# Two graph layers on one core: transfers of the reciprocals split by rows, divisions two steps later, values in pieces

## The chip, the cores and the metric

The kernel runs on one core of a Trainium2 chip. The metric is the device time of one launch in microseconds. The core has five engines with one instruction stream each: TensorE (PE in the profile; PEld is its weight load), VectorE (DVE), ScalarE (ACT), GpSimd (POOL, hardly used here) and SyncE (SP), which here only issues DMA transfers. All transfers run on the core's 16 DMA engines. [...]

## The reference, cut to what matters

Two graph layers run in sequence on `x` of shape (8, 2048, 256), with one adjacency matrix of 2048 x 2048. Each layer is followed by a residual sum and a layer norm.

```
# layer 0, 8 heads of 32 columns, per batch entry
x_proj = x @ W[h];  e = leaky_relu(e_src[i] + e_dst[j], 0.2) + beta * log(adj + 1e-6)
attn   = softmax(where(adj > 0, e, -inf))           # over j
x      = layernorm(x + concat_h(attn @ x_proj) @ W_out.T)
# layer 1, one head of 256 columns
e      = leaky_relu((x W1) (x W2)^T, 0.2);  attn = softmax(where(adj > 0, e, -1e12))
x      = layernorm(x + relu(attn @ (x W3)))
```

What the change touches is the softmax of layer 0. The kernel sums unnormalised products and denominators and divides at the end, by multiplying with the reciprocal of the denominator.

## The kernel before, in words

A batch entry of layer 0 is an object of class `Gat`. It goes through its work in 64 **steps**: four head pairs (`hp`) times 16 column tiles (`jt`) of 128. A step (`Gat.step`) takes a tile `mt` of the transposed edge weights (128 x 2048, 1 MB, loaded from DRAM by `load_mt`), makes one score tile `s` per head on VectorE (L373), and lets TensorE multiply: `val` with the projected values `v`, `den` with the column factors `re` (both L408, in `products`). In some steps the denominator part is added on VectorE instead (L384). There are four buffers for `s`, so VectorE can be two steps ahead of TensorE.

After a head pair's last step, `Gat.finish` takes over. It is a generator: each `yield` ends what is done in one step, and `step` takes the next part of each generator in the list `later` at its start. The parts are: copy the sums out of PSUM (L421, L424); after two steps bring the denominators into a compact shape (`rc`, L428) and take reciprocals (L429); a step later store them to DRAM (`rec_d`, L432). Every second head pair (`lo` is not 0) then has reciprocals of four heads complete, and a step later it brings them back, each row of 1024 broadcast over the 32 partitions of its head, as `rb` (L440, one transfer of 128 x 1024 for each half of the rows), and multiplies the 128 x 1024 halves of `ht` with it (L443). In entry 0 nothing is put off: all parts are run through at once.

There are thus 16 places (8 entries, second and fourth head pair) with two `rb` transfers and two divisions each.

Layer 1 of an entry is an object of class `Dot`, with 16 steps of 128 rows: scores `e` (L530), mask and row maximum on VectorE (L535), exponential on ScalarE (L538), turned blocks (L553, L555), product with `h3` (L569), relu, residual sum and norm (L574, L575, `layer_norm`).

The main loop at the bottom runs layer 1 of one entry together with the steps of the next entry's layer 0. `dot.step(fill)` calls `fill` at three places, and there `layer_0(n)` does n steps. At an entry's end the loop runs the last two dot steps of the entry before, then `output` (product with `W_out`, residual sum, norm; L469 to L482) and `turn` (transposes and `h3`) of the new one, with two steps in each gap. Entry 0 runs beside `others`, a generator that projects the `x` of all other entries (`row`, L270), in the order 2, 3, 4, 5, 1, 6, 7, and stores the values of entries 2 to 7 in DRAM (`v_d`). They are fetched back by `load` (L310) when the entry begins. `others` has two buffers for the values it makes, `v` and `h3`; entries 6 and 7 both use `h3`.

What sets the order: TensorE follows the program's order from the start, and SyncE from line 650 on (all but entry 0), so a SyncE transfer that waits for a buffer holds up the ones after it. The order of VectorE and ScalarE is laid out ahead of time by a planner that works with its own estimates of durations and keeps to it, whatever really comes first.

Buffers with a common tag share slots. The tag `ht` of pool `chunk` has three, for `dn`, `rb`, layer 1's `h1`, the `x` groups of `output` and, in layer 1 of entry 0, the adjacency rows (L212). The tag `d` of pool `wide` has two of 128 x 2048: odd `mt` tiles in entry 0 and in entry 1's first head pair, and later the sums of L384.

Of the kernel before, what the change touches and what calls it, by code (L numbers as in the profile page):

```python
# [9 lines left out]
F32 = mybir.dt.float32  # L10
# [8 lines left out]
P = 128  # L19
# [8 lines left out]
def kernel(  # L28
# [26 lines left out]
    nc = tc.nc  # L55
    B, N, D = x.shape
    H, _, DH = w_proj.shape
    NT = N // P
    KC = D // P
    BK = 512  # L60
    NB = N // BK
    HALF = N // 2
    HP = 2
    NP = H // HP
    IG = BK // P
# [9 lines left out]
    chunk = ctx.enter_context(tc.tile_pool(name="chunk", bufs=2))  # L75
# [4 lines left out]
    def mm_tile(name):  # L80
        return ps.tile([P, BK], F32, tag="mm", name=name)

    def wide_tile(name, tag, bufs, dtype=F32):
        return wide.tile([P, N], dtype, tag=tag, name=name, bufs=bufs)
# [75 lines left out]
    v_d = dram.tile([B, P, NT, D], F32, name="v_d")  # L160
    re_d = dram.tile([B, P, 2, NT, H], F32, name="re_d")
    rec_d = dram.tile([B, NP // 2, 2, 2, 2, HALF], F32, name="rec_d")
    x1_d = dram.tile([B, N, D], F32, name="x1_d")

    def load_x(b, g):

        xg = wide.tile([P, IG, D], F32, tag="pen", name="xg", bufs=1)
        nc.sync.dma_start(xg, x[b].rearrange("(t p) d -> p t d", p=P)[:, ts(g, IG), :])
        return xg
# [64 lines left out]
    class Gat:  # L234
# [72 lines left out]

        def load(self):
            self.v = whole.tile([P, NT, D], F32, name="v")
            nc.sync.dma_start(self.v, v_d[self.b])  # L310

        def load_factors(self):
            self.re = small.tile([P, 2, NT, H], F32, name="re", bufs=3)
# [98 lines left out]
        def finish(self, hp):  # L412

            b, lo = self.b, hp % 2 * HP * DH
            if hp == 0:
                self.ht = whole.tile([P, NT, KC, P], F32, tag="heads", name="ht")
            ht = self.ht[:, :, hp // 2, :]
            for s in range(2):  # L420
                nc.scalar.copy(ht[lo:lo + HP * DH, ts(s, NT // 2), :],  # L421
                               self.val[ts(s, HP * DH), :].rearrange("p (t i) -> p t i", i=P))
            dn = chunk.tile([P, HALF], F32, tag="ht", name="dn", bufs=3)
            nc.scalar.copy(dn, self.den)  # L424
            yield
            yield
            rc = small.tile([P, HALF // DH], F32, name="rc", bufs=1)
            nc.sync.dma_start(rc, dn[::DH, :].rearrange("q (p c) -> q p c", c=HALF // DH))  # L428
            nc.vector.reciprocal(rc, rc)  # L429
            yield  # L430
            for s in range(2):
                nc.sync.dma_start(rec_d[b, hp // 2, s, hp % 2].rearrange("a (p c) -> (a p) c", c=HALF // DH),  # L432
                                  rc[ts(s, HP * DH), :])
            if lo == 0:
                return
            yield
            for s in range(2):
                rb = chunk.tile([P, HALF], F32, tag="ht", name="rb", bufs=3)
                src = rec_d[b, hp // 2, s]
                nc.sync.dma_start(rb, bass.AP(tensor=src.tensor, offset=src.offset,  # L440
                                              ap=[[HALF, 2 * HP], [0, DH], [1, HALF]]))
                half = ht[:, ts(s, NT // 2), :]
                nc.vector.tensor_mul(half, half, rb.rearrange("p (t i) -> p t i", i=P))  # L443

        def output(self):


            b = self.b
            xb = x[b].rearrange("(t p) d -> p t d", p=P)
            xs = []  # L450

            def load(g):
                xs.append(chunk.tile([P, IG, D], F32, tag="ht", name="xg", bufs=3))
                nc.sync.dma_start(xs[g], xb[:, ts(g, IG), :])

            for g in range(NB - 1):
                load(g)
            yield
            for g in range(NB):
                if g == 2:  # L460
                    load(NB - 1)
                st = small.tile([P, IG, nc.vector.BN_STATS_DIM], F32, name="st4", bufs=1)
                mv = small.tile([P, IG, nc.vector.BN_AGGR_DIM], F32, name="mv4", bufs=2)
                z = self.ht[:, ts(g, IG)].rearrange("p t k i -> p t (k i)")
                for k in range(0, IG, 2):
                    y = mm_tile("y").rearrange("p (t c) -> p t c", t=2)
                    for i in range(2):
                        for kc in range(KC):
                            nc.tensor.matmul(y[:, i, :], self.ht[:, g * IG + k + i, kc, :], wot[:, kc, :],  # L469
                                             start=(kc == 0), stop=(kc == KC - 1))  # L470
                    nc.vector.tensor_add(z[:, k:k + 2, :], y, xs[g][:, k:k + 2, :])
                    for i in range(k, k + 2):
                        nc.vector.bn_stats(st[:, i, :], z[:, i, :])
                        nc.vector.bn_aggr(mv[:, i, :], st[:, i, :])
                f = small.tile([P, 2, IG], F32, name="f4", bufs=2)
                nc.scalar.activation(f[:, 0, :], mv[:, :, 1], AF.Ln, bias=eps_ln)
                nc.scalar.activation(f[:, 0, :], f[:, 0, :], AF.Exp, scale=-0.5)
                nc.vector.scalar_tensor_tensor(f[:, 1, :], mv[:, :, 0], -1.0, f[:, 0, :], ALU.mult, ALU.mult)
                for k in range(IG):
                    nc.scalar.activation(z[:, k, :], z[:, k, :], AF.Identity, bias=f[:, 1, k:k + 1],  # L480
                                         scale=f[:, 0, k:k + 1])
                nc.scalar.dma_start(x1_d[b].rearrange("(t p) d -> p t d", p=P)[:, ts(g, IG), :], z)  # L482
                yield
# [115 lines left out]
    def others():  # L599


        order = gats[2:-2] + gats[1:2] + gats[-2:]
        groups = [(gat, g) for gat in order for g in range(NB)]
        xgs, xts = [], []

        def load(n):
            if n < len(groups):
                xgs.append(load_x(groups[n][0].b, groups[n][1]))

        def turn(n):  # L610
            if n < len(groups):
                xts.append(chunk.tile([P, KC, BK], F32, tag="ht", name="xt", bufs=3))
                transpose_x(xgs[n], xts[n])
                load(n + 1)

        load(0)
        turn(0)
        for n, (gat, g) in enumerate(groups):
            turn(n + 1)
            if g == 0:  # L620
                gat.begin("h3" if n // NB % 2 or gat is order[-1] else "v")
            for k in range(IG):
                gat.row(g * IG + k, xts[n])
                if g == NB - 1 and k == IG - 1:
                    gat.factors()
                    for i in range(NB):
                        gat.scale(i)
                    if gat.b > 1:
                        gat.store()
                if g == 0 and k == IG - 1 and n > 0:  # L630
                    groups[n - 1][0].queries()
                yield
        order[-1].queries()
        yield

    projections, weights = others(), later_weights()
    count = (B - 1) * NT
    for k in range(1, NP * NT + 1):
        g0.step()
        if k == NP * NT:  # L640
# [11 lines left out]
    for b in range(1, B + 1):  # L652
        gat, fresh = gats[b - 1], gats[b] if b < B else None

        def layer_0(count):
            if fresh:
                fresh.step(count)

        if b > 1 and fresh:
            fresh.load()  # L660
            fresh.follow(gat)
        rows, turns = gat.output(), gat.turn()
        if dot is None:
            layer_0(4)
            next(rows)
            next(projections)
            layer_0(2)
        else:

            dot.step(lambda k: layer_0((0, 2, 2)[k]))  # L670
            if not fresh:
                for work in gat.later:
                    for _ in work:
                        pass

            def fill(k):
                if k == 1:
                    layer_0(2)
                    next(rows)

            dot.step(fill)

        for g in range(NB + 2):
            if g < NB:
                next(rows)
            if g > 1:
                next(turns)
                next(turns)
            if g < NB + 1:
                layer_0(2)  # L690
        dot = Dot(gat)
        dot.step(lambda k: layer_0((2, 0, 2)[k]))
        count = NP * NT - 20
        for i in range(NT - 3):
            n = (i + 1) * count // (NT - 3) - i * count // (NT - 3)
            dot.step(lambda k: layer_0((0, n - 2, 2)[k]))
# [31 lines left out]
```

## Time and profile before

| | before |
|---|---|
| time, median of 3 runs | 4535.02 us (4534.83 to 4538.08) |
| span of the profiled run | 4539.9 us |
| TensorE busy | 4289.9 us (94%) |
| VectorE busy | 3602.1 us (79%) |
| ScalarE busy | 1660.3 us (37%) |
| granted TensorE clock, mean | 0.978 |
| `mt` loads | 496 of 1024 KB |
| `rb` loads | 32 of 512 KB |
| `v` loads | 6 of 2048 KB |

How to read the lines. A group's line gives line, engine, operation, the tile written and those read, shapes and count, then busy time and mean duration in ns, then the idle time of the engine just before these instructions and what ended it. A line of the timeline gives start and duration in us, and in brackets the idle time before with what ended it. In the table by stretch, each engine's busy time is followed by its instruction count in brackets, and the last three columns are the granted clock of TensorE, the busy share of the 16 DMA engines, and GB/s. A busy TensorE is not TensorE at its peak, for the end of a matmul is modelled, and at half clock the same work shows twice the busy time.

### The profile page before, as it was taken

What the parts mean: (1) busy time and instruction counts of PE and PEld (TensorE: products, weight loads), DVE (VectorE), ACT (ScalarE), POOL (GpSimd) and SP (SyncE); (2) the same over time, 40 slices, a digit from 0 to 9 for tenths busy, and PEclk for the clock granted to TensorE, in tenths of its full rate; (3) what the DMA queues carried; (4) which work ended last, traced back from release to release, by engine and by line L of the source; (5) the groups of instructions that cost most, each with busy time, mean ns of one, the idle gap of its engine ahead of it and who ended that gap; (6) DMA issues with size and microseconds to landing.
All of it is one profiled execution on the core that took longest, in us unless ns stands there. A gap on an engine that the chain in (4) does not pass through costs nothing.

```text
span 4539.9 us, 59623 instructions
## 1 busy us (share of the span) xinstructions
PE 4289.9 (94%) x25072; PEld 2221.2 (49%) x25072; DVE 3602.1 (79%) x2606; ACT 1660.3 (37%) x3019; POOL 9.5 (0%) x14
## 2 busy tenths in 40 slices
PE   7989899998999989998999989999999989999899
PEld 4444354444544445454454444454454544544666
DVE  6878877897789879898789977898798987899222
ACT  6522133332333323333343323333333323333454
POOL 0000000000000000000000000000000000000000
PEclk9999899999999999999999999999999999999999
DMA  8877656555455554555545454455544455453211
GB/s 253 295 245 265 244 191 204 216 201 203 167 183 187 200 201 151 180 187 201 187 176 187 167 202 174 178 188 197 198 170 165 178 206 182 177 182 141 74 49 40
DMA packets 248652, 839.07 MB, mean 185 GB/s; under 512 B 30016, under 2 KB 148544, under 8 KB 173120
## 3 DMA queue, kind: packets, MB, share of 16 engines
q1 hardware_dynamic: 213056, 801.71, 49.9%
q10 hardware_dynamic: 35328, 33.56, 2.2%
q8 instruction: 196, 3.21, 0.3%
q14 instruction: 72, 0.59, 0.0%
HBM read 761.53 MB, written 73.14 MB: 184 GB/s over the span
## 4 chain that ended last, share of the span: by engine, by line
PE 47%; DVE 20%; DMA 10%; issue 8%; ACT 3%; SPq 0%; DVEq 0%; ACTq 0%
DVE s L373 13%; PE e L530 12%; PE acc L569 12%; PE val L408 9%; PE den L408 6%; DMA rb<-rec_d 5%; DMA mt<-mt_d 4%; DVE d L384 3%; PE pt L553 3%; PE h1p L520 2%; PE h3p L500 2%; DVE p L535 1%; PE y L469 1%; ACT d L390 1%; ACT p L538 1%
## 5 line engine op out<-in xcount | busy, mean ns | idle before, releaser
L373 DVE SCALAR_TENSOR_TENSOR s<-c,re,mt 128x2048 f32<-128x2048 f32 x1024 | 2354.6, 2342 | 205.7 <-PE den L408 147.1
L408 PE MATMUL val<-s,v 128*32 128x512 f32 x8192 | 1064.0, 613 | 136.6 <-DVE s L373 134.6
L569 PE MATMUL acc<-h,pts 128*128 128x256 f32 x4096 | 956.4, 381 | 26.8 <-ACT pts L555 26.8
L530 PE MATMUL e<-x1t,h 128*128 128x512 f32 x2048 | 909.4, 596 | 16.4 <-ACT pts L555 7.7
L569 PEld LDWEIGHTS acc<-h,pts 128*128 128x128 f32 x4096 | 748.2, 190 | 125.1 <-ACT pts L555 39.2
L408 PE MATMUL den<-s,re 128*32 128x512 f32 x5648 | 712.7, 598 | 0.0
L408 PEld LDWEIGHTS val<-s,v 128*32 128x32 f32 x8192 | 245.7, 111 | 788.0 <-issue 520.7
L384 DVE SCALAR_TENSOR_TENSOR d<-s,re,d 128x2048 f32<-128x2048 f32 x264 | 615.0, 2344 | 0.0
L530 PEld LDWEIGHTS e<-x1t,h 128*128 128x128 f32 x2048 | 380.3, 191 | 472.6 <-issue 414.8
L555 ACT COPY pts<-pt 128x512 f32<-128x512 f32 x512 | 296.1, 582 | 766.1 <-PE pt L553 758.7
L535 DVE CUSTOM_DVE_ANT_0 p<-p,pen 128x2048 f32<-128x2048 f32 x128 | 292.8, 2287 | 249.6 <-ACT p L532 237.8
L532 ACT ACTIVATE p<-e 128x512 f32<-128x512 f32 x512 | 302.9, 595 | 440.6 <-PE e L530 433.2
L408 PEld LDWEIGHTS den<-s,re 128*32 128x32 f32 x5648 | 194.0, 111 | 432.1 <-issue 427.4
L553 PEld LDWEIGHTS pt<-ident,p 128*128 128x128 f32 x2048 | 239.5, 141 | 229.0 <-issue 180.4
L538 ACT ACTIVATE p<-p,neg 128x2048 f32<-128x2048 f32 x128 | 256.7, 2005 | 234.6 <-DVE neg L535 234.6
L553 PE MATMUL pt<-ident,p 128*128 128x128 f32 x2048 | 320.6, 279 | 5.1 <-ACT p L538 5.1
L574 ACT ACTIVATE z<-acc,rec 128x256 f32<-128x256 f32 x128 | 60.6, 473 | 393.2 <-PE acc L569 274.3
L575 DVE TENSOR_TENSOR z<-z,x1r 128x256 f32<-128x256 f32 x128 | 54.0, 422 | 164.5 <-ACT z L574 164.3
L443 DVE TENSOR_TENSOR ht<-ht,rb 128x1024 f32<-128x1024 f32 x32 | 39.2, 1225 | 155.2 <-DMA rb<-rec_d 155.2
L270 PE MATMUL proj<-wp,xt 128*128 128x272 f32 (+1 forms) x512 | 135.8, 409 | 19.8 <-ACT both L274 10.1
L500 PE MATMUL h3p<-w3s,x1t 128*128 128x256 f32 x512 | 123.3, 384 | 14.2 <-ACT x1t L495 13.7
L224 ACT ACTIVATE f<-mv,eps_ln 128x1 f32<-128x1 f32 x128 | 37.8, 295 | 250.1 <-DVE mv L222 250.0
(89 smaller groups left out, 2016.3 us busy)
## 6 DMA issues: line engine op xcount, KB each, us to landing
mt<-mt_d SPq DMA_DIRECT2D x496, 1024.0 KB
c<-c_d SPq DMA_DIRECT2D x64, 1024.0 KB
pen<-pen_d SPq DMA_DIRECT2D x112, 512.0 KB
xg<-in_x_dram SPq DMA_DIRECT2D x60, 512.0 KB
adj_t<-in_adj_dram SPq DMA_DIRECT2D x16, 1024.0 KB
mt_d<-mt SPq DMA_DIRECT2D x16, 1024.0 KB
rb<-rec_d SPq DMA_DIRECT2D x32, 512.0 KB
x_d<-ht ACTq DMA_DIRECT2D x32, 512.0 KB
```

Source lines behind the costliest of these rows:

```text
L270: nc.tensor.matmul(t[:, 0:cols], xt[:, kc, ts(it % IG, P)], wp[:, kc, 0:cols], start=(kc == 0), stop=(kc == KC - 1))
L373: nc.vector.scalar_tensor_tensor(sa, self.cs[a], self.re[:, 0, jt, h:h + 1], mt, ALU.max, ALU.mult)
L384: nc.vector.scalar_tensor_tensor(d, sa, e[:, jt - 1, h:h + 1], d, ALU.mult, ALU.add)
L408: nc.tensor.matmul(dst[ts(q, DH), ts(c, BK)], weights[q % 2], s[q % 2][:, ds(q // 2 * HALF + c * BK, BK)], start=start, stop=stop)
L500: nc.tensor.matmul(t[:, ts(i, D)], x1t[:, kc, ts(2 * (j - 1) + i, P)], w3s[:, kc, :], start=(kc == 0), stop=(kc == KC - 1))
L530: nc.tensor.matmul(t, self.h1[:, kc, ts(it % IG, P)], self.x1t[:, kc, ts(c, BK)], start=(kc == 0), stop=(kc == KC - 1))
L532: nc.scalar.activation(p[:, ts(c, BK)], t, AF.Prelu, alpha=ALPHA)
L535: nc.vector.tensor_tensor_reduce(p, p, pen, -1.0, FMAX, ALU.add, ALU.min, neg)
L538: nc.scalar.activation(p, p, AF.Exp, bias=neg, scale=-1.0, accum_out=den)
L553: nc.tensor.transpose(t[:, ts(k, P)], p[:, ts(g * IG + k, P)], ident)
L555: nc.scalar.copy(pt, t)
L569: nc.tensor.matmul(acc, now[:, ts(k, P)], self.h3[:, j, :], start=(j == 0), stop=(j == NT - 1))
```

## The change

Five edits, all about when things are fetched and used:

1. **Reciprocals in four transfers a half.** Instead of one transfer of 128 x 1024 with a source of four rows, each repeated 32 times, there are four, each of one row to the 32 partitions of its head. In entry 0 the tile is taken from the tag `d` instead of `ht`.
2. **Divisions two steps behind.** The transfers of half 0 are issued in one step, those of half 1 in the next, then the divisions follow in one step each.
3. **Values in four pieces.** `load` becomes a generator; the first 512 KB are asked for at once, the others one a step.
4. **The x groups of `output`** are asked for one ahead instead of three at the start.
5. **Entry 0.** The first `x` group of `others` is asked for before the first step; the transposes of the next group come after the second row of the present one; ahead of entry 7 there are four turns with no row, so that entry 6's values can be stored first. The counts of steps are fitted to that.

```
         def load(self):
             self.v = whole.tile([P, NT, D], F32, name="v")
-            nc.sync.dma_start(self.v, v_d[self.b])
+            for g in range(NB):
+                nc.sync.dma_start(self.v[:, ts(g, IG), :], v_d[self.b, :, ts(g, IG), :])
+                yield
...
             yield
+            rbs = []
             for s in range(2):
-                rb = chunk.tile([P, HALF], F32, tag="ht", name="rb", bufs=3)
-                src = rec_d[b, hp // 2, s]
-                nc.sync.dma_start(rb, bass.AP(tensor=src.tensor, offset=src.offset,
-                                              ap=[[HALF, 2 * HP], [0, DH], [1, HALF]]))
+                if b == 0:
+                    rb = wide_tile("rb", "d", 2)[:, 0:HALF]
+                else:
+                    rb = chunk.tile([P, HALF], F32, tag="ht", name="rb", bufs=3)
+                for a in range(2 * HP):
+                    nc.sync.dma_start(rb[ts(a, DH), :],
+                                      rec_d[b, hp // 2, s, a // HP, a % HP:a % HP + 1, :].to_broadcast([DH, HALF]))
+                rbs.append(rb)
+                yield
+            for s, rb in enumerate(rbs):
                 half = ht[:, ts(s, NT // 2), :]
                 nc.vector.tensor_mul(half, half, rb.rearrange("p (t i) -> p t i", i=P))
+                yield
...
-            for g in range(NB - 1):
-                load(g)
+            load(0)
+            load(1)
             yield
             for g in range(NB):
-                if g == 2:
-                    load(NB - 1)
+                if 0 < g < NB - 1:
+                    load(g + 1)
...
         load(0)
+        yield
         turn(0)
         for n, (gat, g) in enumerate(groups):
-            turn(n + 1)
             if g == 0:
+                if gat is order[-1]:
+                    for _ in range(IG):
+                        yield
                 gat.begin("h3" if n // NB % 2 or gat is order[-1] else "v")
             for k in range(IG):
                 gat.row(g * IG + k, xts[n])
+                if k == 1:
+                    turn(n + 1)
...
-    count = (B - 1) * NT
+    next(projections)
+    count = (B - 1) * NT + IG
...
         if b > 1 and fresh:
-            fresh.load()
             fresh.follow(gat)
+            values = fresh.load()
+            next(values)
+            fresh.later.append(values)
...
             layer_0(4)
             next(rows)
             next(projections)
-            layer_0(2)
...
-        count = NP * NT - 20
+        count = NP * NT - (18 if b == 1 else 20)
```

## The prediction

> **What bounds the kernel now.** I read the page first, for the engines and the idle time:
>
> ```profile
> PE 4289.9 (94%) x25072; PEld 2221.2 (49%) x25072; DVE 3602.1 (79%) x2606; ACT 1660.3 (37%) x3019; POOL 9.5 (0%) x14
> ...
> PE 47%; DVE 20%; DMA 10%; issue 8%; ACT 3%; SPq 0%; DVEq 0%; ACTq 0%
> DVE s L373 13%; PE e L530 12%; PE acc L569 12%; PE val L408 9%; PE den L408 6%; DMA rb<-rec_d 5%; DMA mt<-mt_d 4%; DVE d L384 3%; PE pt L553 3%; PE h1p L520 2%; PE h3p L500 2%; DVE p L535 1%; PE y L469 1%; ACT d L390 1%; ACT p L538 1%
> ...
> L443 DVE TENSOR_TENSOR ht<-ht,rb 128x1024 f32<-128x1024 f32 x32 | 39.2, 1225 | 155.2 <-DMA rb<-rec_d 155.2
> ```
>
> TensorE (PE) is the bound: 4540 - 4290 = 250 us of its span are idle, so no change of waits alone can save much more than that. The chain spends 5% in the transfers of the reciprocals, `rb<-rec_d`. The last line says how: all 32 divisions (L443) found VectorE (DVE) idle in front of them, 155.2 us in sum, each time for that transfer. VectorE time is not TensorE time, so I went to the timeline of one such place, the end of entry 2's last head pair: VectorE, then TensorE, then the DMA share by stretch.
>
> ```profile
> 1580.24 0.15 DVE L572 RECIPROCAL rec<-den 128x1 f32<-128x1 f32 x1
> 1590.41 1.23 DVE L443 TENSOR_TENSOR ht<-ht,rb 128x1024 f32<-128x1024 f32 x1 [10.01 <-DMA rb<-rec_d]
> 1591.55 0.42 DVE L575 TENSOR_TENSOR z<-z,x1r 128x256 f32<-128x256 f32 x1
> 1591.89 2.35 DVE L373 SCALAR_TENSOR_TENSOR s<-c,re,mt 128x2048 f32<-128x2048 f32 x1
> 1595.48 1.23 DVE L443 TENSOR_TENSOR ht<-ht,rb 128x1024 f32<-128x1024 f32 x1 [1.24 <-DMA rb<-rec_d]
> ```
>
> ```profile
> 1594.29 1.91 PE L408 MATMUL val<-s,v 128*32 128x512 f32 x2 [6.33 <-DVE s L373]
> 1599.35 4.13 PE L408 MATMUL val<-s,v 128*32 128x512 f32 x16 [3.15 <-DVE s L373]
> ```
>
> ```profile
> 1576.25 1.23 SPq L440 DMA_DIRECT2D rb<-rec_d  x2
> ```
>
> ```profile
> 1588.00:1592.00 4.00, 0.00 (x0) 0.00 (x0) 1.59 (x3) 0.58 (x1) 0.00 (x0) 1.00 0.28 87
> 1592.00:1596.00 4.00, 1.71 (x2) 0.18 (x2) 2.76 (x2) 0.00 (x0) 0.00 (x0) 0.62 0.26 108
> ```
>
> The two transfers of 512 KB are issued at 1576.25 and only landed for the division at 1595.48, 19 us later. VectorE stands in program order in front of the divisions, the score tiles (L373) queue behind them, and TensorE waits 6.33 + 3.15 us for those. The last three columns are granted clock, DMA share and GB/s: while only `rb` is under way, the DMA share is 0.26 to 0.28, about 4 engines of 16, at 108 GB/s. The clock falls to 0.62: TensorE restarts at half clock after the gap. (On the page the clock is 0.978 on average; if the other state is 0.5, 0.022 / 0.5 x 4540 = 200 us run at half clock.)
>
> **What the Trainium skill says.** "DMA: Bandwidth & Descriptors", section "Why a DMA increments its semaphore by 16 and not by 1": a transfer uses the largest count of engines up to 16 that divides the slowest dimension of both sides. The old source leads with 4 rows, the destination with 128 partitions: 4 engines. The trace agrees (0.26 of 16). The new ones lead with 32 on both sides: 16 engines. The same page, "Rules for kernel authors", advises against cutting a transfer by partitions, because the parts share the same engines; that does not hold against a whole that is confined to four. "TensorE: Matmul & The Clock Gate", section "HAM oscillation — how this bites in real kernels", puts the price of a gap at half of the throttled time; the trace shows the halved clock at 1592 to 1600.
>
> **The change part by part.**
>
> *Reciprocals on 16 engines.* 1 MB in 2 transfers at 108 GB/s is 9.7 us alone, and 19 us as it shares its four engines with `mt`. On sixteen, at 4 x 108 = 432 GB/s, it is 1.2 us a half, plus a landing delay: the 8 KB `rec_d` stores issued to 1574.8 released the `rb` issue at 1576.25, so 1.5 us. SyncE (SP) issues 8 instead of 2 transfers; the price of one is between 0.32 us (`mt`) and 0.56 us (`rb`), so 2.6 to 4.5 us a pair. I take 0.5. The first half should land by about 1576.3 + 2 + 1.2 + 1.5 = 1581.
>
> *Divisions two steps behind.* The division of half 0 now comes after the score tiles of the next two steps. One step of L373 is 4.6 us, so it stands at about 1580.3 + 4.6 = 1585, four us after the landing; half 1 stands one step later. All 11.2 us of wait at this place should go. Over all 16 places the two waits of each add up as: last head pairs (entries 1 to 7) 10.7, 11.2, 10.8, 11.1, 10.5, 13.7, 8.8; second head pairs 13.8, 7.1, 7.5, 7.3, 7.6, 9.6, 6.8; entry 0 10.5 and 8.1; sum 155.
>
> What that is worth on TensorE:
> - Last head pairs. In 1580 to 1655 (75 us) TensorE is busy 61.3 us and VectorE 58.5, clock 0.91. Full clock would take about 4.6 off TensorE, giving 56.7. So with no wait the stretch is bound by VectorE at some 61 us with its small gaps, 14 us less at most; VectorE's own wait alone is 11.2. I take 12.5 for entries 2 to 6 (62), 11 for entry 1, and 5 for entry 7, where nothing but entry 7's own TensorE gap (3.9 us) and its slow restart are at stake. Sum 78.
> - Second head pairs. TensorE idles 2.1 to 2.9 us (2.5 at 1332.8), then 1.9 us more on `e` because ScalarE stands behind a norm whose VectorE half was late, and restarts at half clock for 3.4 us (1.7 us lost): 6.2 each, six times, and 10 for entry 1 (gap 7.7). Sum 47.
> - Entry 0, two places: TensorE gaps 8.0 and 11.7. The first goes nearly whole, since `xt` no longer waits for the buffer of `rb`; of the second I take half, for entry 1's first odd `mt` tiles now wait for the `d` buffers that `rb` holds. Sum 14.
>
> *Values in four pieces.* 2 MB at once delays the `mt` and `pen` behind it (VectorE waits 2.56 and 2.38 us there). The TensorE wait for `v` is 1.7 us in all, so I count this within the 12.5 above.
>
> *Gap ahead of entry 7.* Its first row shares a buffer with entry 6, whose store starts at 454.38:
>
> ```profile
> 461.50 2.18 PE L270 MATMUL proj<-wp,xt 128*128 128x272 f32 x4 [6.55 <-ACT both L274]
> ...
> 63.86 1.94 PE L175 MATMUL tr<-ident,xg 128*128 128x128 f32 x8 [6.58 <-DMA xg<-in_x_dram]
> ```
>
> Four empty turns are over two steps (some 12 us) of other TensorE work: 6.55 us and the slow restart, 8. At the start, the second load still follows the first transposes; only two rows of 0.9 us now lie between: 2.
>
> *Costs.* 96 more issues x 0.5 = 48 us of SyncE time. SyncE waits for VectorE over 2000 us at L202, so most of it is hidden; I charge 1 us a place, 16. In entry 1 the mask tiles (L212) share the three `ht` buffers with `rb`, held two steps longer, and SyncE is in order: `mt` loads queue behind a blocked mask load. Between nothing and two steps of 4.6 us; I take 8. Splitting `output`'s x loads is free: the later ones land behind a step's score tiles.
>
> Sum: 78 + 47 + 14 + 8 + 2 - 16 - 8 = 125. **4535 - 125 = 4410 us.**
>
> **Rivals.**
> - *Everything comes back* (chance 0.15): all 112 us of TensorE gaps around the 16 places (added up from its timeline), half of the 79 us it then works at half clock (its busy time in those stretches of the clock record), the 2.5 us gap seven times in the output stage, and the 10 above, without costs: 112 + 40 + 17 + 10 = 179, so 4356. For it: over 1600 to 2100 as a whole TensorE is busy 487.5 of 500 us, so little else stands in its way. Against: in the output stage VectorE has as much work as TensorE.
> - *The wait moves on* (0.22): `mt` transfers and in-order VectorE take over, and only half is kept: 125 / 2 = 62, so 4473. For it: 43 us of `mt` waits stand already, and VectorE's order is laid out by a planner that does not know real landings. Against: many of those `mt` waits are `rb`'s doing on the four shared engines.
> - *Slower* (0.08): every half delays an `mt` by its 2 us of issue (64 us), mask loads in entry 1 cost two steps at each of its places (20), and half of the first gain remains (62): 4535 + 64 + 20 - 62 = 4557.
> - Same within 0.2%: 0.03. My forecast: 0.52.
>
> **How the numbers follow.** The predicted time is the forecast's. Low: near the first rival, 4365. High: past the second, 4485, which leaves out the slower case. Faster 0.89, same 0.03, slower 0.08.
>
> **What would show it.** After: the 155 us at L443 are near nothing; `rb` has 128 issues of 128 KB; TensorE's busy time falls by some 40 us as restarts vanish, its idle time by some 90; mean clock rises to about 0.985 or more; the TensorE gap at L270 for entry 7 is gone. The prediction is wrong if `rb` still runs on four engines, if the planner puts the divisions ahead of the landings again, or if the waits of L373 for `mt` grow from 43 us to over 100.

## The result, and the profile after

| | before | after |
|---|---|---|
| time, median of 4 runs each | 4534.93 us (4531.48 to 4538.08) | 4412.79 us (4410.09 to 4415.41) |
| span of the profiled run | 4539.9 us | 4410.4 us |
| TensorE busy / idle in its span | 4289.9 / 250.0 us | 4248.7 / 161.7 us |
| mean granted clock | 0.978 | 0.989 |
| stretches at half clock, sum (of it TensorE busy) | 195.8 us (128.5) | 93.5 us (65.6) |
| VectorE waits for `rb` / for `mt` | 155.2 / 43.3 us | 7.0 / 59.6 us |

The ratio of the times is 0.9731 (95% interval 0.9714 to 0.9748): 122 us less. The prediction was 4410. The two profiled executions lie further apart, 129.5 us by their spans: that of the kernel before took 4541.7 us, more than any of its four runs here. The sums from traces below add up to that 129.5. From line 310 on, the line numbers moved: L373 is now L375, L384 is L386, L408 is L410, the `rb` issue L440 is L446, the division L443 is L452, `e` L530 is L540, `acc` L569 is L579.

The page after: engines, the chain that ended last by line, the costliest VectorE group, and the `rb` issues.

```profile
PE 4248.7 (96%) x25072; PEld 2215.7 (50%) x25072; DVE 3603.8 (82%) x2606; ACT 1663.4 (38%) x3019; POOL 9.5 (0%) x14
...
DVE s L375 14%; PE e L540 13%; PE acc L579 12%; PE val L410 10%; PE den L410 7%; DMA mt<-mt_d 4%; PE pt L563 3%; DVE d L386 3%; DMA rb<-rec_d 2%; PE h3p L510 2%; PE h1p L530 1%; PE y L479 1%; DVE p L545 1%; ACT d L392 1%; ACT p L548 1%
...
L375 DVE SCALAR_TENSOR_TENSOR s<-c,re,mt 128x2048 f32<-128x2048 f32 x1024 | 2354.2, 2342 | 218.6 <-PE den L410 141.0
...
rb<-rec_d SPq DMA_DIRECT2D x128, 128.0 KB
```

Not one instruction was taken off TensorE (25072 on both pages), and VectorE does the same 3.60 ms of work. TensorE's idle time fell by 88 us and its busy time by 41. The work of TensorE is the same, so most of the 41 is clock. At half clock the same products show twice the time: sixteen of `val` take 4.13 us in the prediction's line at 1599.35, which lies at half clock but for its last 0.3 us, and 1.92 us at 1528.21 in the trace after, at full clock. By the clock records of the traces, 63 us less of TensorE's busy time lie at half clock, and half of that, some 31 us, is time saved; the remaining 10 us I can't place. On VectorE, what its score tiles (L375) wait for most is `den`, that is TensorE's release of an `s` buffer, as it was before (147.1 us then, 141.0 now). The `rb` transfers fell from 5% of the chain to 2%.

The view of the tile `rb`, after: how the transfers were issued (min, median, max ns), and what VectorE waited for ahead of the divisions.

```profile
L446 SPq DMA_DIRECT2D rb<-rec_d x128: 302/419/1423, 265.1 to 4081.5; - x128
L452 DVE TENSOR_TENSOR ht<-ht,rb x32: 1212/1218/1226, 294.8 to 4090.7; 128x1024 f32<-128x1024 f32 x32
its engine sat idle before it (us, times) until:
  DMA rb<-rec_d: 7.0, 1
```

Of 32 waits one is left, and its first start, 294.8, tells where: entry 0. The place that the prediction showed, entry 2's end, in the timeline after; VectorE, then TensorE, then SyncE:

```profile
1546.19 4.61 DVE L375 SCALAR_TENSOR_TENSOR s<-c,re,mt 128x2048 f32<-128x2048 f32 x2 [0.89 <-DMA mt<-mt_d]
1550.72 1.22 DVE L452 TENSOR_TENSOR ht<-ht,rb 128x1024 f32<-128x1024 f32 x1
1551.86 2.35 DVE L386 SCALAR_TENSOR_TENSOR d<-s,re,d 128x2048 f32<-128x2048 f32 x1
1554.12 4.61 DVE L375 SCALAR_TENSOR_TENSOR s<-c,re,mt 128x2048 f32<-128x2048 f32 x2
1558.64 2.35 DVE L386 SCALAR_TENSOR_TENSOR d<-s,re,d 128x2048 f32<-128x2048 f32 x1
1560.91 1.22 DVE L452 TENSOR_TENSOR ht<-ht,rb 128x1024 f32<-128x1024 f32 x1
```

```profile
1550.86 1.92 PE L410 MATMUL val<-s,v 128*32 128x512 f32 x14 [0.35 <-DVE s L375]
1556.52 1.92 PE L410 MATMUL val<-s,v 128*32 128x512 f32 x2 [3.75 <-DVE s L375]
```

```profile
1537.08 1.97 SPq L446 DMA_DIRECT2D rb<-rec_d  x4
...
1546.16 2.14 SPq L446 DMA_DIRECT2D rb<-rec_d  x4
```

Each division has a step of score tiles (4.61 us) ahead of it and starts with no bracket, that is without a wait. TensorE still waits 3.75 us here, but for another reason: while it can go no further without score tiles, VectorE does a division and a sum (L386) between them, 3.6 us of its own work. The two issues of four are a step apart, and neither is waited for.

### The profile page after: what moved, and what is told of

Its sections match the earlier page's. It is cut to its first block, busy times and chain, and to the rows that moved or that the text cites. A ratio compares the mean times of both kernels' runs of the same rounds, so it can differ in the third digit from the quotient of the medians.

```text
span 4410.4 us, 59810 instructions
## 1 busy us (share of the span) xinstructions
PE 4248.7 (96%) x25072; PEld 2215.7 (50%) x25072; DVE 3603.8 (82%) x2606; ACT 1663.4 (38%) x3019; POOL 9.5 (0%) x14
## 4 chain that ended last, share of the span: by engine, by line
PE 50%; DVE 21%; issue 7%; DMA 7%; ACT 3%; SPq 1%; DVEq 0%; ACTq 0%
DVE s L375 14%; PE e L540 13%; PE acc L579 12%; PE val L410 10%; PE den L410 7%; DMA mt<-mt_d 4%; PE pt L563 3%; DVE d L386 3%; DMA rb<-rec_d 2%; PE h3p L510 2%; PE h1p L530 1%; PE y L479 1%; DVE p L545 1%; ACT d L392 1%; ACT p L548 1%
## 5 line engine op out<-in xcount | busy, mean ns | idle before, releaser
L375 DVE SCALAR_TENSOR_TENSOR s<-c,re,mt 128x2048 f32<-128x2048 f32 x1024 | 2354.2, 2342 | 218.6 <-PE den L410 141.0
L410 PE MATMUL val<-s,v 128*32 128x512 f32 x8192 | 1044.3, 605 | 90.7 <-DVE s L375 90.5
L579 PE MATMUL acc<-h,pts 128*128 128x256 f32 x4096 | 953.8, 380 | 12.1 <-ACT pts L565 12.1
L540 PE MATMUL e<-x1t,h 128*128 128x512 f32 x2048 | 905.2, 594 | 8.0 <-ACT h L532 8.0
L579 PEld LDWEIGHTS acc<-h,pts 128*128 128x128 f32 x4096 | 747.5, 190 | 107.4 <-ACT pts L565 22.1
L410 PE MATMUL den<-s,re 128*32 128x512 f32 x5648 | 706.1, 594 | 0.0
L386 DVE SCALAR_TENSOR_TENSOR d<-s,re,d 128x2048 f32<-128x2048 f32 x264 | 615.3, 2345 | 0.0
L540 PEld LDWEIGHTS e<-x1t,h 128*128 128x128 f32 x2048 | 379.4, 190 | 460.3 <-issue 415.8
L410 PEld LDWEIGHTS val<-s,v 128*32 128x32 f32 x8192 | 245.1, 110 | 723.0 <-issue 510.5
L410 PEld LDWEIGHTS den<-s,re 128*32 128x32 f32 x5648 | 192.7, 110 | 426.0 <-issue 420.0
L270 PE MATMUL proj<-wp,xt 128*128 128x272 f32 (+1 forms) x512 | 130.9, 401 | 3.2 <-ACT v L272 1.8
L272 ACT COPY v<-proj 128x256 f32<-128x256 f32 x128 | 47.0, 376 | 211.4 <-PE proj L270 197.5
L479 PE MATMUL y<-wot,ht 128*128 128x256 f32 x512 | 117.6, 383 | 0.0
```

What stands on the lines that cost most here:

```text
L375: nc.vector.scalar_tensor_tensor(sa, self.cs[a], self.re[:, 0, jt, h:h + 1], mt, ALU.max, ALU.mult)
L386: nc.vector.scalar_tensor_tensor(d, sa, e[:, jt - 1, h:h + 1], d, ALU.mult, ALU.add)
L410: nc.tensor.matmul(dst[ts(q, DH), ts(c, BK)], weights[q % 2], s[q % 2][:, ds(q // 2 * HALF + c * BK, BK)], start=start, stop=stop)
L540: nc.tensor.matmul(t, self.h1[:, kc, ts(it % IG, P)], self.x1t[:, kc, ts(c, BK)], start=(kc == 0), stop=(kc == KC - 1))
L579: nc.tensor.matmul(acc, now[:, ts(k, P)], self.h3[:, j, :], start=(j == 0), stop=(j == NT - 1))
```

## Where the gain came from, by stage

The pages give totals. To place them, I read from each trace when TensorE starts the score products of a given step, since from entry 2 on the work before that point is the same in all these kernels, and took the difference to the kernel before (each from one profiled execution). The columns `e1`, `e2`, `e9`, `e10` are experiments told below.

| gain over before, us | after | e1 | e2 | e9 | e10 |
|---|---|---|---|---|---|
| entry 0, step 32 | 5.2 | -2.9 | 3.2 | 3.4 | 1.6 |
| entry 0, step 40 (past its first place) | 1.5 | 9.0 | -11.6 | 12.2 | 9.9 |
| end of entry 0 | 7.4 | 10.0 | -4.8 | 19.0 | 16.8 |
| entry 2, step 20 | 30.9 | 38.5 | -15.2 | 45.4 | 48.1 |
| end | 129.5 | 137.3 | 42.5 | 143.0 | 149.4 |
| of it from entry 2, step 20, on | 98.6 | 98.8 | 57.7 | 97.6 | 101.3 |

Within those 98.6 us of the change, the second head pairs of entries 2 to 7 gained 7.0, 7.4, 7.3, 7.5, 9.4 and 6.7 (45.3), the last head pairs with the output stage behind them 8.1, 9.9, 11.2, 7.2 and 12.1 in entries 2 to 6 (48.5), and 4.8 in entry 7. In entry 0 the change *lost* 3.7 us at the first division (5.2 to 1.5).

## The experiments

Twelve kernels ran, each beside the kernel before on the same chip. All ratios are to the kernel before. My theory was that both halves of the `rb` edit count: sixteen engines make the landing early, and two steps put VectorE's work in front of it. The rivals were that one of them does all of it, and that the delay only costs.

**e1: the kernel before, with the transfers split and nothing else.**

```
-                src = rec_d[b, hp // 2, s]
-                nc.sync.dma_start(rb, bass.AP(tensor=src.tensor, offset=src.offset,
-                                              ap=[[HALF, 2 * HP], [0, DH], [1, HALF]]))
+                for a in range(2 * HP):
+                    nc.sync.dma_start(rb[ts(a, DH), :],
+                                      rec_d[b, hp // 2, s, a // HP, a % HP:a % HP + 1, :].to_broadcast([DH, HALF]))
```

> The kernel before, with nothing changed but the reciprocals: four transfers of one row to 32 partitions for each half, divisions still in the same step. Theory (the number of engines is what was wrong): each half lands some 2 and 5 us after VectorE is ready instead of 10 and 15, so the waits in front of the divisions fall from 155 us to about 45 and the time to about 4465 (4445 to 4485). Rival (what matters is only that the divisions come later; the speed of the transfer is hidden or eaten by its six more issues): 4520 to 4540, waits above 110 us.

Measured: 4400.17 us, ratio 0.9692 (0.9678 to 0.9707). Its interval lies below that of the whole change, and no division waits. My expectation missed. The reason stands in its timeline, the same place on VectorE:

```profile
1538.12 4.62 DVE L373 SCALAR_TENSOR_TENSOR s<-c,re,mt 128x2048 f32<-128x2048 f32 x2 [0.26 <-PE val L408]
1542.66 1.22 DVE L443 TENSOR_TENSOR ht<-ht,rb 128x1024 f32<-128x1024 f32 x1
1543.79 4.60 DVE L384 SCALAR_TENSOR_TENSOR d<-s,re,d 128x2048 f32<-128x2048 f32 x2
1548.32 1.21 DVE L443 TENSOR_TENSOR ht<-ht,rb 128x1024 f32<-128x1024 f32 x1
```

The program puts the divisions where they were, yet VectorE's instructions now stand in another order: before, the first division came right behind a small reciprocal (`rec`, L572, 0.15 us); here a step of score tiles stands ahead of it and two sums between the two. The planner lays VectorE's order out from its own estimates, and with eight transfers in place of two it came to this one. Why it did is not to be seen in a trace. So "split only" is in effect also "divisions later", and e1 doesn't measure the sixteen engines by themselves.

Its trace does allow an estimate for this place. From 1534 to 1538 us only `rb` is under way:

```profile
1534.00:1538.00 4.00, 4.00 (x31) 2.26 (x33) 1.35 (x5) 0.57 (x2) 0.00 (x0) 1.00 1.04 236
```

A share of about 1 says that all sixteen engines are at work, where it was 0.26 to 0.28 before. The rate is 236 GB/s, a little over twice that of the four engines and not the four times (432) of the prediction, so a half takes 2.2 us and not 1.2; why an engine moves less here is open. The last DMA packet of the first half ends at 1536.1 and that of the second at 1538.6. Had the division stayed right behind `rec`, which ends at 1534.3, it would have waited some 2 to 3 us by these figures, in place of 10.01. The engines thus do most of the work at this place, and the new order the rest; that is an estimate, and no run holds the order fixed.

**e2: the change, with one transfer a half again** (the same three lines put back). The delay stays, and the four engines are back; the other edits of the change stay too.

> The changed kernel, but each half comes in one transfer as before (source of four rows). Theory (engine count): a pair of halves still needs 10 us alone and up to 19 beside the mt loads, two steps cover 5 to 10 of them, so 60 to 100 us of waits are back in front of the divisions, mt loads wait on the four shared engines, and the time is about 4465 (4440 to 4490). Rival (the delay of two steps is enough by itself): 4410 to 4425, waits below 20 us.

Measured: 4496.82 us, ratio 0.9904 (0.9889 to 0.9919). The tile view of `rb`:

```profile
  DMA rb<-rec_d: 80.5, 14
```

Without the split, the delay halves the waits: 80.5 us at 14 divisions in place of 155.2 at 32. In the second head pairs of entries 2 to 7 none is left, in the last ones of entries 2 to 6 some 6 us each. There the planner has left the first division where it stood before, ahead of two score tiles that it follows in the change. By the table it gains 57.7 us from entry 2, step 20, on and loses 15 up to there; entry 0, where the divisions aren't put off, has two TensorE gaps of 23 and 26 us. The first of them:

```profile
317.43 1.92 PE L410 MATMUL val<-s,v 128*32 128x512 f32 x2 [23.16 <-DVE s L375]
```

The direction was right; the loss against the change (84 us) was larger than expected, above my range, and entry 0 is what I had not counted.

**e3: the change, with two transfers of two rows each.** Count of transfers between 1 and 4, engines fewer than either.

```
-                for a in range(2 * HP):
-                    nc.sync.dma_start(rb[ts(a, DH), :],
-                                      rec_d[b, hp // 2, s, a // HP, a % HP:a % HP + 1, :].to_broadcast([DH, HALF]))
+                for a in range(2):
+                    src = rec_d[b, hp // 2, s, a]
+                    nc.sync.dma_start(rb[ts(a, HP * DH), :], bass.AP(tensor=src.tensor, offset=src.offset,
+                                      ap=[[HALF, HP], [0, DH], [1, HALF]]))
```

> The changed kernel, but each half comes in two transfers of two rows, each row to 32 partitions. Theory (a transfer uses as many engines as its outermost count, 2): both transfers run on the same two engines, DMA share 0.13 while only they are under way, about 20 us for a pair of halves at 54 GB/s, worse than one transfer a half: 4500 (4470 to 4540). Rival (it is the number of transfers that brings the speed): between the changed kernel and the one with a single transfer, 4415 to 4440.

Measured: 4616.17 us, ratio 1.0171 (1.0154 to 1.0188): slower than before. The direction was mine, the size not: I had 4540 at most. A stretch in which only `rb` is under way (last columns: clock, DMA share, GB/s), the division that waits there, and the tile view:

```profile
1622.00:1626.00 4.00, 2.41 (x16) 0.47 (x14) 0.43 (x1) 0.41 (x1) 0.00 (x0) 1.00 0.13 51
```

```profile
1626.85 1.22 DVE L454 TENSOR_TENSOR ht<-ht,rb 128x1024 f32<-128x1024 f32 x1 [4.41 <-DMA rb<-rec_d]
...
1642.72 1.23 DVE L454 TENSOR_TENSOR ht<-ht,rb 128x1024 f32<-128x1024 f32 x1 [3.56 <-DMA rb<-rec_d]
```

```profile
  DMA rb<-rec_d: 184.9, 32
```

The share of 0.13 is two engines of sixteen (2/16 = 0.125), at 51 GB/s; before it was 0.26 to 0.28 at 87 to 108 GB/s. The Trainium skill, "DMA: Bandwidth & Descriptors", section "Why a DMA increments its semaphore by 16 and not by 1", says that the slowest dimension of both sides sets the count of engines; a source that leads with two rows gives two, and the two transfers of one half ran on the same two. So it is the leading count that counts, not that there are more transfers: one transfer with 4 rows gives 4497, two with 2 rows 4616, four whose sides both lead with 32 give 4413, with the delay in all three. This comes closer to the clean test that e1 isn't: in entries 2 to 7 all 24 divisions of e3 stand behind as many score tiles and sums as in the change, and from entry 2, step 20, on alone e3 is 138 us behind it. (Only e2 has another order there, in the last head pairs.)

**e4: the change, with entry 0's divisions put off step by step as in the other entries.**

```
-            self.later = gats[b - 1].later if b > 1 else []
+            self.later = gats[b - 1].later if b > 0 else []
...
-                    if self.b == 0:
-                        for _ in work:
-                            pass
-                    else:
-                        self.later.append(work)
+                    self.later.append(work)
```

(with the two steps that the change drops behind entry 0's `output` put back, and the count of steps of entry 1 at 20)

> The changed kernel, but entry 0's divisions are put off step by step like those of the other entries (and the two steps ahead of entry 0's output are back in place). In the changed kernel TensorE idles 11.1 us at 292 and 12.2 us at 496, in front of entry 0's two divisions. Theory (the planner sets both divisions ahead of the next score tiles because they are asked for in the same step): the gaps shrink to below 5 us each, 4398 (4390 to 4406). Rival (the gaps come from the d buffers that the reciprocals take from the odd mt tiles): the same gaps, 4408 to 4418.

Measured: 4406.92 us, ratio 0.9709 (0.9693 to 0.9724). The two TensorE gaps of 11 and 12 us became one of 6.3 and six of 0.9 to 4.0 (11 in sum), but the interval overlaps that of the change. Inconclusive; its sign is as expected, its size is not.

**e5: the change again**, as the base on the chip that ran e6 to e8.

> The changed kernel once more, as the standard for the runs beside it on the same chip: 4412 (4406 to 4420).

Measured: 4413.31 us, ratio 0.9723 (0.971 to 0.9737).

**e6: the change without its edits to `others`** (first `x` group at once, the transposes behind the second row, four empty turns ahead of entry 7).

```
-            if gat is order[-1]:
-                for _ in range(IG):
-                    yield
...
-    next(projections)
-    count = (B - 1) * NT + IG
+    count = (B - 1) * NT
```

> The changed kernel, with the generator of the other entries' projections as in the kernel before (no early first x, second transposes at once, no four empty turns ahead of entry 7). Theory: the TensorE gaps of 6.6 us at the start and 6.5 us ahead of entry 7 are back, where the changed kernel has 4.3 and 4.2, each with a slow restart: 4 to 8 us slower than the changed kernel. Rival (entry 0 has slack, or the gap only moves): within 3 us of it.

Measured: 4421.48 us, ratio 0.9744 (0.973 to 0.9757), 8.2 us above e5, with intervals that just overlap. The TensorE gaps are 7.8 us at the start and 6.5 us ahead of entry 7, where e5 has 5.2 and 4.2: 5 us in sum. Another 3.5 us come from the gaps at entry 0's two divisions, 13.0 and 14.1 us in place of 11.4 and 12.1. So the edits gain about what I had (8 + 2), but not all of it at the two gaps that they aim at; these shrink and don't vanish.

**e7: the change with the values in one transfer of 2 MB.**

```
-            for g in range(NB):
-                nc.sync.dma_start(self.v[:, ts(g, IG), :], v_d[self.b, :, ts(g, IG), :])
-                yield
+            nc.sync.dma_start(self.v, v_d[self.b])
+            yield
```

> The changed kernel, with the values of an entry in one transfer of 2 MB. Theory (hidden: the entry's first steps have mt tiles in hand and TensorE has layer 1 work): within 4 us of the changed kernel, though VectorE's waits for mt rise from 60 us by 10 to 20. Rival (the mt tiles behind the 2 MB are on the path, since the divisions follow right after): 8 to 20 us slower than it.

Measured: 4408.94 us, ratio 0.9714 (0.97 to 0.9727): no loss, as expected. The waits for `mt`, which I thought would rise by 10 to 20, fell: 62.9 us in e5, 47.7 here.

**e8: the change with three `x` groups of `output` asked for at the start again.**

```
-            load(0)
-            load(1)
+            for g in range(NB - 1):
+                load(g)
...
-                if 0 < g < NB - 1:
-                    load(g + 1)
+                if g == 2:
+                    load(NB - 1)
```

> The changed kernel, with three x groups of the output stage asked for at once. Theory: the third waits for the buffer of the second division's reciprocals, and SyncE, in order, holds the mt loads behind it until that division is done, one step later; VectorE then waits some 2 us for mt at seven entry ends: 5 to 15 us slower than the changed kernel. Rival (mt is two steps ahead, so the hold is covered): within 4 us of it.

Measured: 4412.07 us, ratio 0.9721 (0.9708 to 0.9734): no difference to e5. My theory missed and the rival held.

**e9: the change with entry 0's `rb` in the `ht` buffers.** Entry 0 was where the change lost time, and it is the only place where `rb` sits in a `d` buffer.

```
-                if b == 0:
-                    rb = wide_tile("rb", "d", 2)[:, 0:HALF]
-                else:
-                    rb = chunk.tile([P, HALF], F32, tag="ht", name="rb", bufs=3)
+                rb = chunk.tile([P, HALF], F32, tag="ht", name="rb", bufs=3)
```

> The changed kernel, with the one difference that entry 0's reciprocals lie in the three ht buffers, as in the other entries, and not in the two d buffers. In the changed kernel TensorE idles 11 and 12 us in front of entry 0's divisions, against some 1 and 5 to 9 in the kernel before with split transfers alone. Theory (the d buffers: odd mt tiles cannot be loaded while reciprocals hold them, and the divisions go first): the gaps shrink to below 6 us each and the time to 4400 (4394 to 4406). Rival (asking for both halves and then dividing both is what puts the divisions in front of the score tiles): the gaps stay above 9 us, 4408 to 4418.

Measured: 4401.23 us, ratio 0.9691 (0.9674 to 0.9707): 12 us less than e5 by the medians. By the table its gain is 1.8 us behind that of the change at step 32 and 10.7 ahead at step 40, so about 12.5 us come between these two, where the first division stands. VectorE at that place, first in the change, then in e9:

```profile
294.85 2.36 DVE L452 TENSOR_TENSOR ht<-ht,rb 128x1024 f32<-128x1024 f32 x2 [7.02 <-DMA rb<-rec_d]
300.91 9.14 DVE L375 SCALAR_TENSOR_TENSOR s<-c,re,mt 128x2048 f32<-128x2048 f32 x4 [3.71 <-DMA mt<-mt_d]
```

```profile
294.05 4.62 DVE L375 SCALAR_TENSOR_TENSOR s<-c,re,mt 128x2048 f32<-128x2048 f32 x2 [1.45 <-PE den L410]
298.58 2.35 DVE L449 TENSOR_TENSOR ht<-ht,rb 128x1024 f32<-128x1024 f32 x2
302.59 13.66 DVE L375 SCALAR_TENSOR_TENSOR s<-c,re,mt 128x2048 f32<-128x2048 f32 x6 [1.66 <-DMA mt<-mt_d]
```

In the change the two `rb` tiles take both `d` buffers, which odd `mt` tiles use in entry 0. VectorE waits 7.02 us for `rb`, divides, and then waits 3.71 us for `mt`. With `rb` elsewhere, two score tiles stand ahead of the divisions, and the wait for `rb` is gone. TensorE's two gaps fall from 11.1 and 12.2 us to 1.9 and 5.6. That the `d` tag does it is shown. SyncE in the change shows for how long the buffers are held:

```profile
265.14 0.33 SPq L446 DMA_DIRECT2D rb<-rec_d  x1
...
280.28 0.78 SPq L446 DMA_DIRECT2D rb<-rec_d  x2
...
291.25 1.71 SPq L446 DMA_DIRECT2D rb<-rec_d  x4
296.10 1.95 SPq L202 DMA_DIRECT2D mt<-mt_d  x3
```

Split by rows, a half no longer waits as a whole: the rows of the first head pair are in DRAM already, and SyncE, which is free of the program's order in entry 0, fetches them from 265.14 on, 22 us before the second pair's reciprocals are taken (287.48). From then until the divisions end at 297.2 the `d` buffers are taken, and of `mt` tiles one is asked for between 265 and 296. VectorE's order fits: in the change 66 score tiles stand ahead of the first division, in the kernel before and in e9 70. That the planner stepped aside for `mt` in particular is still my reading of these lines.

**e10: the kernel before, with the split of e1 and the edits to `others`, and nothing else.**

> The kernel before with two parts of the change: the split transfers and the rearranged projections beside entry 0; divisions in the same step, values whole, x groups three at once. Theory (the split alone was worth 140 us, the projections 8, and the two steps of delay nothing once the transfers are fast): 4392 (4386 to 4399), faster than the whole change by some 20. Rival (the gains do not add, for the projections only moved a gap): 4400 to 4412.

Measured: 4394.83 us (4388.44 to 4396.37), ratio 0.9678 (0.9664 to 0.9693). The lowest of all, though its interval overlaps those of e1 and e9; it lies below that of the change (0.971 to 0.9737 in e5; 0.9714 to 0.9748 in the first comparison).

**e11 and e12: the sums moved out of the divisions' way.** In e1 TensorE keeps a gap at entry 2's end, for the score tiles behind two divisions and two sums:

```profile
1551.85 1.92 PE L408 MATMUL val<-s,v 128*32 128x512 f32 x2 [7.14 <-DVE s L373]
```

So I moved the sums of that head pair from steps 4 and 5 to 12 and 13, in e10 (e11) and in the change (e12):

```
-    SUMMED += [[(2, 4, 5)] + [(1, 3, 5, 7, 9, 11, 13)] * (NP - 1)] * (B - 2)
+    SUMMED += [[(2, 12, 13)] + [(1, 3, 5, 7, 9, 11, 13)] * (NP - 1)] * (B - 2)
```

> As the split with the projections, but the denominator sums of the first head pair of entries 2 to 7 that VectorE takes over from TensorE are those of column tiles 12 and 13 instead of 4 and 5, so that they no longer stand beside the divisions. Theory (with the transfer out of the way, the 7.1 us gap of TensorE at each of five entry ends is VectorE's work: two score tiles, two divisions and two sums in a row): the gap falls below 3 us, 25 to 40 us faster than without, 4362 (4350 to 4372). Rival (the output stage, which follows, has no room on VectorE, so the wait only moves): within 8 us of it.

> The whole change, with the same sums moved to column tiles 12 and 13. Theory (VectorE's work in a row, as with the split alone): its gaps of 3.7 and 1.7 us at each entry end go, 15 to 30 us faster than the change, 4390 (4380 to 4400). Rival: within 8 us of the change.

Measured: e11 4405.05 us, ratio 0.9703 (0.969 to 0.9717); e12 4421.45 us, ratio 0.974 (0.9724 to 0.9756). Both some 8 to 10 us slower than their bases; this theory fell. In e11 the gap of 7.1 us did shrink, to 2.1, and against e10 each entry gained 5 to 8 us up to step 14. In the next two steps it lost 9 to 10. VectorE and TensorE of e11 at the end of entry 3's first head pair:

```profile
1612.61 4.61 DVE L384 SCALAR_TENSOR_TENSOR d<-s,re,d 128x2048 f32<-128x2048 f32 x2
1617.13 6.87 DVE L373 SCALAR_TENSOR_TENSOR s<-c,re,mt 128x2048 f32<-128x2048 f32 x3
```

```profile
1619.54 1.04 PE L408 MATMUL val<-s,v 128*32 128x512 f32 x2 [3.16 <-DVE s L373]
1621.80 2.78 PE L408 MATMUL val<-s,v 128*32 128x512 f32 x11 [1.22 <-DVE s L373]
```

The sums, 4.61 us of VectorE, stand there ahead of the score tiles, and TensorE waits for those. The gap was moved, not removed. In e12 it is the same: against the change, each entry gained 7 to 9 us up to step 14 and lost 8 to 11 in the next two. Another 6 us were lost ahead of entry 2, where no sum was moved; that stays open.

## Why the prediction was right, and where its terms were not

**The bound and the mechanism: right.** The waits of the divisions went from 155.2 us to 7.0, `rb` has 128 issues of 128 KB, idle time fell by 88 (foretold: some 90) and busy time by 41 (some 40), the clock is 0.989 (0.985 or more), and the gap at L270 ahead of entry 7 is gone, though one of 4.2 us at L410, for a score tile, stands in its place. e3 shows that the count of engines is the cause of the transfers' part. The rate on sixteen engines was taken at 432 GB/s and was 236 (e1); a half that took 2.2 us instead of 1.2 was still in time.

**Last head pairs, 78, of which 62 in entries 2 to 6: too much.** Measured 48.5. The step took the stretch to be bound by VectorE at 61 us and gave back all of its wait. But the change leaves a gap of TensorE in it, 3.75 us behind a division and a sum in entry 2. Entry 7 gave 4.8 of 5.

**Second head pairs, 47, of which 37 in entries 2 to 7: too little.** Measured 45.3, so 7.5 each instead of 6.2. Their gaps fell to nothing (0.5 us on `e` is left in entry 2), and with them one that the sum left out: 1.8 us on `acc` (L569) behind each of these places, at 1356.7 in entry 2.

**Entry 0, 14: wrong.** This is the step that failed. "The first goes nearly whole, since `xt` no longer waits for the buffer of `rb`": its gap grew instead, from 8.0 to 11.1 us, and the second went from 11.7 to 12.2. I had seen that the `d` buffers keep odd `mt` tiles waiting, but charged that to entry 1 alone; in entry 0 it stands at once, the more so as half of the rows are fetched 22 us early (e9). e9 puts it at 12 us by the times; with the `ht` buffers the two gaps are 1.9 and 5.6 us, together 12 less than before, and the 14 would have been about right.

**Costs, 16 + 8: they hardly appeared.** An issue takes 0.42 us at the median (I took 0.5), and the 128 of them take 58 us of SyncE in place of 18, but in e10, which has the same 128, nothing was lost: it gains 101.3 us from entry 2 on. While the mask tiles are loaded beside entry 1 (520 to 1100 us in both traces), VectorE's waits for `mt` did rise by as much as I charged, from 15.3 us to 24.4. Not all of it reached the time: from the end of entry 0 to entry 2, step 20, e9, with the delay, gains 26.4 us and e10, without it, 31.3, so some 5 of the 8 at most. Up to entry 2, step 20, the change gained 30.9 us; the working gives 33 for it (2 + 8 + 14 + 11 + 10, less 8 and less 4 for issues), so most of what entry 0 lost came back in these terms and in entry 1's own places.

**Gap ahead of entry 7 and start, 10: right in size.** e6 measures 8.2, of which some 5 at these two gaps.

**Values and x groups, nothing: right** (e7 and e8).

**What the sum hid.** The prediction treats sixteen engines and two steps of delay as two remedies that work together. They are two for one illness. From entry 2, step 20, on the delay without the split gives 57.7 us (e2), the split without the programmed delay 98.8 (e1), and both together 98.6. With the split, the programmed delay adds nothing to the order that the planner finds by itself. The change also puts entry 0's `rb` into the `d` buffers, which cost 12 us, and that accounts for most of the 18 us by which e10 is better than the change. The rest, some 6 us, is not told apart. The forecast hit in part by luck, because its errors cancelled: 13 too much and 8 too little in the head pairs of entries 2 to 7, some 15 too much in entry 0, some 20 too little from costs that were hardly paid.

**The rivals.** "Everything comes back" (4356) failed on the 161.7 us that are still idle: its terms (112 + 17 + 10) would have left some 110 of the 250. "The wait moves on" (4473) is seen in small: waits for `mt` rose from 43.3 to 59.6 us, and TensorE kept gaps at the divisions. The slower case would have needed the issues to be on the path; by e10 they are not.

## What to carry to other kernels

When a wait names a transfer, look at the share of the DMA engines while it runs alone: a share that stays near 4/16 or 2/16 says that the shape of the access, not the bytes, sets the time, and the leading count on both sides is the thing to change, not the number of transfers. And a share near 1 doesn't promise four times the rate of four engines: measure it. Of two remedies for one wait, try each alone before you add them up; the second may bring nothing but its own side effects. And when a tile moves to another tag, ask for every user of that tag what it will now wait for, in the very entry where it is moved.

## What the runs showed that I had not expected

- Two transfers of two rows each are slower than one of four rows: 51 GB/s on two engines, against 87 to 108 on four, and 184.9 us of waits against 80.5. The Trainium skill's "Rules for kernel authors" in "DMA: Bandwidth & Descriptors", which advises against cutting a transfer by partitions because the parts share all sixteen engines, fits the outcome of this cut (+2.7% against e2) and not that of the one into four (-1.9% against e2): the leading count tells which.
- A split of transfers changed the order of VectorE's work, which no line of the edit touches (e1). A planner that works from estimates answers to a transfer's shape too.
- Sixteen engines moved the split rows at 236 GB/s, where four had moved the whole at 87 to 108.
- A gap of TensorE can cost twice: beside 88 us of idle time, 63 us less of TensorE's work ran at half clock, some 31 us more by the estimate above.
